# A second round for m and its transpose in the far lanes of a Newton-Schulz kernel, and side queues that skip finished entries

## The chip, the cores and the metric

The kernel runs on one core of a Trainium2 chip. The metric is the device time of one execution in microseconds; lower is better.

## The reference, cut to what matters

The input x is 32 images of 32 channels of 128 x 128. Layer 0 takes a group norm of x, then five steps of a Newton-Schulz iteration for the matrix square root of every one of the 1024 matrices A, and adds the result to x. Layer 1 takes a group norm of that, a spectral convolution on the lowest 32 modes, and adds again.

```
Y = A / norm(A);  Z = I
for _ in range(5):
    T = 0.5 * (3 I - Z @ Y);  Y = Y @ T;  Z = T @ Z
x = x + Y * sqrt(norm(A))                  # layer 0, A = group_norm(x)
F = real(fft2(group_norm(x)))              # layer 1
F = einsum over input channels of F[low modes] with weights1, weights2
x = x + real(ifft2(F, zeros elsewhere))
```

## The kernel before

The kernel doesn't run the five steps as written: `newton` (L388 to L411) computes the same kind of polynomial with two quartic stages and a last product. Its unit is a **quad**: four channels of one image, four 128 x 128 matrices side by side in a tile of 128 x 512 fp32. There are 256 quads. One product of a quad (`products`, L298) is four fp32 matrix products, which the trace shows as 8 matmul records; `transposed` (L304) shows as 4.

**One quad.** `quartic` computes v = products(mb, m) and then q = products(v, w), where w is v transposed plus r. In `newton` the first quartic gives q; then y = products(q, m); then the new m = products(q, y); then mb, the transpose of m, and r = mb + identity; then the second quartic; then two products (L298 names them m,q and y,q), the product named q,t, and the last one, y,t, which is added to xt (L410). ACT copies y, m, mb and t from PSUM (`taken`, L267). DVE makes v, q and the second t (`plus`, L273). POOL makes r (L285) and, in far lanes, w (L376).

**Two ways to transpose v.** In images 1 to 19 ("far", `is_far`) DVE transposes 32 x 32 blocks (L360), SP stores the tile to DRAM (L362), loads it in the order wanted (one load in the first quartic, L373; four in the second, L370), and POOL adds r. In the other images ("near") PE transposes v. The far way saves PE work and takes longer. 152 quads are far, 104 near.

**Rounds and lanes.** All of this is unrolled in Python, and the order of the program is the order in which it is written. `newton` is a generator; each `yield` ends a step. The main loop goes in rounds, and in each round each of seven lanes takes one step of its quad. A far quad has 20 steps, and a new one starts every `FAR` = 20/7 rounds, so that all seven lanes are in use; a near quad has 13, starts every 13/4 rounds and uses four lanes. Each engine takes its instructions in the order of the program, so that the number of rounds between a product and the product that uses it decides how much work of other quads lies between them.

**Side work.** Between the lanes' steps the loop gives one turn a round to each of several queues of generators, through `step`: `preps` (statistics of the next image, at lane 1), `specs` (spectrum of a finished image, lane 2), `posts` (`settle`, which stores a finished quad and folds it, and `forward`, the first Fourier transform, lane 3), `prods` (products with the weights) and `backs` (`inverse`, lane 0; `backs` has no turn in every fifth round for most of the time). `norms` (the normalization of the next quad) has a turn before each lane. Images are grouped in 21, 8 and 3 (`GROUPS`); the products of a group start when its last image has its spectrum, and the inverses follow. `step` runs the first generator of a queue up to its next `yield`; a generator that has nothing left to do is taken off the queue, and that uses up the turn.

**Buffers.** `four` gives out tiles by tag in turn; far quads have some more (`rooms`: first number, and what far quads have in addition).

Of the kernel before, what the change touches and what calls it, by code (L numbers as in the profile page):

```python
# [36 lines left out]
C = 32  # L37
G = 16
LANES, LESS = 7, 4
FAR, NEAR = 20 / 7, 13 / 4  # L40
GROUPS = (21, 8, 3)


# [22 lines left out]
def conv_preact_kernel(  # L66
# [74 lines left out]
    def bank():  # L141
        return ps8.tile([P, 4, P], F32, tag="ps", name="ps")
# [111 lines left out]
    def four(tag, far):  # L254
        n, more = rooms[tag]
        if far:
            turns[tag] += 1
            if turns[tag] % (n + more) >= n:
                return early.tile([P, 4, P], F32, tag=tag + "_early", name=tag, bufs=more)
        return sets.tile([P, 4, P], F32, tag=tag, name=tag, bufs=n)  # L260

    def taken(ps, tag, far, f=1.0):
        t = four(tag, far)
        if f == 1.0:
            nc.scalar.copy(t, ps)
        else:
            nc.scalar.mul(t, ps, f)  # L267
        return t

    def plus(ps, f, t, tag, far):  # L270

        s = four(tag, far)
        nc.vector.scalar_tensor_tensor(s, ps, f, t, ALU.mult, ALU.add)  # L273
        return s

    def blocks(t):


        return t.rearrange("p c x -> p (c x)").rearrange("p (a c j) -> p a c j", a=4, c=4)

    def plus_eye(mb, far):

        r = four("r", far)
        if far:
            nc.gpsimd.tensor_tensor(  # L285
                blocks(r).rearrange("p a c j -> p c a j"),
                mb.rearrange("p c (a j) -> p c a j", a=4),
                eye.rearrange("p c (a j) -> p c a j", a=4),
                ALU.add,
            )  # L290
        else:
            nc.gpsimd.tensor_tensor(r, mb, eye, ALU.add)  # L292
        return r

    def products(lhsT, rhs):
        ps = bank()
        for j in range(4):
            nc.tensor.matmul(ps[:, j, :], lhsT[:, j], rhs[:, j], start=True, stop=True)  # L298
        return ps

    def transposed(t):
        ps = bank()
        for j in range(4):
            nc.tensor.transpose(ps[:, j, :], t[:, j, :], ident)  # L304
        return ps

    def is_far(b):
        return 0 < b < FIRST
# [42 lines left out]
    def quartic(m, mb, r, far, wide):  # L351


        v = plus(products(mb, m), -1 / (QA * QR * QS), m, "v", far)
        if far:


            t = four("turn", far)
            form = "p c (b i) -> p b c i" if wide else "p c (i b) -> p b c i"
            nc.vector.transpose(blocks(t), v.rearrange(form, b=4))  # L360
            held = dram.tile([P, 512], F32, name="turn", tag="turn", bufs=8)
            kept(nc.sync.dma_start(out=held, in_=t.rearrange("p c x -> p (c x)")))  # L362
            yield
            w = four("w", far)
            wb = blocks(w).rearrange("p a c j -> p a (c j)")
            if wide:
                for b in range(4):
                    rows = slice(32 * b, 32 * b + 32)
                    src = held[:, P * b : P * b + P].rearrange("(a i) x -> i a x", a=4)
                    kept(nc.sync.dma_start(out=wb[rows], in_=src))  # L370
            else:
                src = held.rearrange("(a i) (b x) -> (i b) a x", a=4, b=4)
                kept(nc.sync.dma_start(out=wb, in_=src))  # L373
            yield
            yield
            nc.gpsimd.tensor_tensor(w, w, r, ALU.add)  # L376
            w = blocks(w).rearrange("p a c j -> p c a j")
        else:
            yield
            w = plus(transposed(v), 1.0, r, "w", far)  # L380
        yield
        q = plus(products(v, w), 1 / (16 * QS * QS), eye, "q", far)
        yield
        if far:
            yield
        return q

    def newton(g, sn, xt, m, mb, r, far):  # L388


        q = yield from quartic(m, mb, r, far, False)
        y = taken(products(q, m), "y", far, 1 / MS)
        yield
        m = taken(products(q, y), "m", far, MS)
        yield
        mb = taken(transposed(m), "mb", far, QR * QS / MS)
        r = plus_eye(mb, far)
        yield
        q = yield from quartic(m, mb, r, far, True)
        pw, py = products(q, m), products(q, y)  # L400
        w, y = taken(pw, "t", far, 1 / MS), four("y4", far)
        for j in range(4):
            c = 4 * g + j
            nc.scalar.mul(y[:, j, :], py[:, j, :], sn[:, c : c + 1])  # L404
        yield
        t = plus(products(w, q), -0.5 * EYE / 1.5, eye, "t", far)
        yield
        if far:
            yield
        nc.vector.tensor_tensor(xt, products(t, y), xt, ALU.add)  # L410
        yield  # L411
# [128 lines left out]
    def wide_products(i):  # L540
# [5 lines left out]
        def load(step):  # L546
            kk, h = divmod(step, 2)
            for l4 in range(4):
                rows = slice(32 * l4, 32 * l4 + 32)
                kept(nc.sync.dma_start(out=wts[h][rows, l4], in_=wk[kk, rows, h]))  # L550
            if not h:
                kept(nc.sync.dma_start(out=xks[kk % 2][:, 0:n, :], in_=xs[i][kk, :, 0:n, :]))
# [14 lines left out]
        for step in range(2 * KK):  # L567
            yield
            kk, h = divmod(step, 2)
            wt, xk = wts[h], xks[kk % 2]  # L570
            if not h:
                om = page(f"om{i}_{kk}")
            pm = bank()
            for t in range(4):
                for q in range(4):
                    nc.tensor.matmul(  # L576
                        pm[32 * q : 32 * q + 32, t, :],
                        xk[:, :, 8 * q + 4 * h + t],
                        wt[:, :, q, t, :],
                        start=True,  # L580
                        stop=True,
                    )
            nc.scalar.copy(
                om.rearrange("p (o l) -> p o l", l=L)[:, :, 16 * h : 16 * h + 16],
                pm.rearrange("p t (l o) -> p o (t l)", l=4),
            )
            if done and not h:
                store(*done)
            if h:
                done = kk, om  # L590
            if step + 2 < 2 * KK:
                load(step + 2)
# [208 lines left out]
    backs = []  # L801

    def step(queue):
        if queue and next(queue[0], queue) is queue:
            queue.pop(0)


# [60 lines left out]
    while todo or any(lanes) or posts or specs or prods or backs:  # L868
# [10 lines left out]
        for i in range(LANES):  # L879
            step(norms)  # L880
            far = todo and is_far(todo[0][0])
            room = lanes[i] is None and (far or LANES - lanes.count(None) < LESS)
            if todo and room and rounds >= due:
                due = max(due, rounds - 1) + (FAR if far else NEAR)
                while norms:
                    step(norms)
                b, g = todo.pop(0)
                xt = ready[0][0]
                lanes[i] = (b, g, xt, newton(g, made[b][3], *ready.pop(0), far))
                if stages:  # L890
                    stage()
            if lanes[i] is not None:
                b, g, xt, steps = lanes[i]
                if next(steps, lanes) is lanes:
                    lanes[i] = None
                    end(b, g, xt)
            if i == 1:
                step(preps)
            if i == 2 or tail:
                step(specs)  # L900
            if i == 3 or tail:
                step(posts)
            if i == 0 or tail:
                step(prods)
            if i == 0 and (rounds % 5 or len(ended) > B - 6) or tail and not (posts or specs):
                step(backs)
# [65 lines left out]
```

## Time and profile before

The median of three runs is 3214.82 us (3211.49 to 3221.01). The profiled execution has a span of 3216.0 us.

| engine | busy us | share |
|---|---|---|
| PE (matmul) | 2973.3 | 92% |
| DVE | 2365.3 | 74% |
| POOL | 2008.4 | 62% |
| ACT | 1716.3 | 53% |

A row of the page's groups gives line, engine, operation, output and inputs, shape and count, then busy us and the mean ns of one, then the engine's idle time before them and what ended most of it. A row of the waits gives the waiting engine, tile and line, what it waited for, the total in us, how many times, and the longest. In time, the profile falls into the far stage (from about 105 to 1780 us), the near stage (to about 3095 us; the products of the first group lie at 1900 to 2100 us, their inverses from 2050 to 2800), and a tail of about 120 us with the last group's products and inverses.

### The profile page before, as it was taken

Reading aid. Unit: us, or ns where it says so; the run is one execution under the profiler, and the core shown is the slowest. Engines: PE = TensorE matmul, PEld = TensorE weight load, DVE = VectorE, ACT = ScalarE, POOL = GpSimd, SP = SyncE. Lnnn points to the kernel's source line nnn. Section 1 sums busy time; section 2 is a strip of 40 time slices with the busy share of each in tenths; the row PEclk is TensorE's granted clock in tenths of the full one; section 3 lists DMA queues with packets and bytes.
Section 4 is the critical chain, followed back from the end, with each engine's and each line's share of the span. In section 5 each row is a group of like instructions: output and inputs, shape, how many; then the busy total and the mean of one; then the engine's idle time right before and its main releaser. Section 6 shows DMA issues by size and latency. Waiting matters only on the chain.

```text
span 3216.0 us, 78946 instructions
## 1 busy us (share of the span) xinstructions
PE 2973.3 (92%) x29440; PEld 2836.6 (88%) x29440; DVE 2365.3 (74%) x5672; ACT 1716.3 (53%) x4148; POOL 2008.4 (62%) x2312
## 2 busy tenths in 40 slices
PE   6999999999999999999999999999999998999954
PEld 6889899899999999999999998898889888999853
DVE  5787788778888887888788665577767776756645
ACT  3555555565556655565565555455555544546533
POOL 3566666666767666666676553466767767746642
PEclk9999999999999999999999999999999999999975
DMA  3466566666666666666666336765767676576667
GB/s 122 148 190 190 192 201 202 186 199 204 196 208 200 210 191 196 207 204 200 191 211 193 96 96 207 227 214 185 232 201 243 213 240 208 193 225 209 207 238 255
DMA packets 482317, 637.55 MB, mean 198 GB/s; under 512 B 97936, under 2 KB 263056, under 8 KB 481936
## 3 DMA queue, kind: packets, MB, share of 16 engines
q1 hardware_dynamic: 366448, 413.30, 40.3%
q10 hardware_dynamic: 113472, 211.86, 21.1%
q0 software_dynamic: 2016, 7.34, 0.6%
q8 instruction: 235, 3.85, 0.5%
q14 instruction: 146, 1.20, 0.1%
HBM read 398.75 MB, written 233.57 MB: 197 GB/s over the span
## 4 chain that ended last, share of the span: by engine, by line
PE 67%; DVE 13%; DMA 12%; ACT 3%; issue 2%; POOL 1%; SPq 1%; ACTq 0%; DVEq 0%; POOLq 0%
PE ps L298 55%; PE ps L304 6%; DMA xs<-in_xt 5%; DMA turn<-turn 2%; PE ps L764 1%; DMA w<-turn 1%; DVE a_st L193 1%; PE ps L442 1%; DVE turn L360 1%; DVE q L273 1%; DVE yt L781 1%; DVE v L273 1%; PE ps L576 1%; PE ps L742 1%; DVE xt L410 1%
## 5 line engine op out<-in xcount | busy, mean ns | idle before, releaser
L298 PE MATMUL ps<-w,v 128*128 128x128 f32 x4096 | 548.5, 278 | 26.4 <-POOL w L376 14.1
L376 POOL TENSOR_TENSOR w<-w,r 128x512 f32<-128x512 f32 x304 | 386.7, 1275 | 270.5 <-DMA w<-turn 222.0
L298 PE MATMUL ps<-y,q 128*128 128x128 f32 x4096 | 549.6, 278 | 3.9 <-ACT y L267 2.2
L423 POOL TENSOR_TENSOR fold<-xt 128x256 f32<-128x256 f32 x512 | 363.7, 731 | 279.2 <-DVE xt L410 262.5
L328 ACT ACTIVATE b<-b,a_off,a_scr 128x128 f32<-128x128 f32 x1024 | 463.9, 489 | 129.7 <-issue 54.8
L298 PEld LDWEIGHTS ps<-w,v 128*128 128x128 f32 x4096 | 500.5, 193 | 35.2 <-POOL w L376 20.1
L298 PEld LDWEIGHTS ps<-y,q 128*128 128x128 f32 x4096 | 504.7, 194 | 7.0 <-ACT y L267 3.3
L273 DVE SCALAR_TENSOR_TENSOR q<-ps,eye 128x512 f32<-128x512 f32 x512 | 347.0, 678 | 99.5 <-PE ps L298 97.9
L717 POOL TENSOR_TENSOR yt<-yt,d 128x512 f32<-128x512 f32 x236 | 297.9, 1289 | 188.0 <-ACT d L776 155.0
L193 DVE BATCH_NORM_STATS2 a_st<-xs 128x6 f32<-128x128 f32 x1024 | 231.8, 279 | 143.4 <-DMA xs<-in_xt 143.0
L335 POOL TENSOR_SCALAR x<-xt,a_nm,a_sc 128x128 f32<-128x128 f32 x720 | 317.8, 454 | 23.9 <-DVE a_n L222 20.8
L404 ACT ACTIVATE y<-ps,a_t_s 128x128 f32<-128x128 f32 x1024 | 292.1, 369 | 62.3 <-PE ps L298 61.5
L292 POOL TENSOR_TENSOR r<-b,eye 128x512 f32<-128x512 f32 x104 | 132.8, 1277 | 283.8 <-issue 224.6
L298 PE MATMUL ps<-m,q 128*128 128x128 f32 x2048 | 280.3, 280 | 27.9 <-DVE q L273 27.6
L298 PE MATMUL ps<-m,mb 128*128 128x128 f32 x2048 | 282.4, 282 | 19.6 <-ACT mb L267 19.6
L273 DVE SCALAR_TENSOR_TENSOR v<-ps,x 128x512 f32<-128x512 f32 x256 | 175.5, 686 | 165.0 <-PE ps L298 162.9
L273 DVE SCALAR_TENSOR_TENSOR v<-ps,m 128x512 f32<-128x512 f32 x256 | 174.7, 683 | 162.8 <-PE ps L298 162.1
L298 PE MATMUL ps<-y,t 128*128 128x128 f32 x2048 | 280.6, 281 | 6.6 <-DVE t L273 4.5
L298 PEld LDWEIGHTS ps<-m,q 128*128 128x128 f32 x2048 | 252.1, 194 | 35.4 <-DVE q L273 17.9
L360 DVE STREAM_TRANSPOSE turn<-v 128x512 f32<-128x512 f32 x304 | 277.9, 914 | 7.2
L298 PE MATMUL ps<-x,b 128*128 128x128 f32 x2048 | 275.6, 278 | 5.6 <-POOL x L335 5.6
L298 PEld LDWEIGHTS ps<-m,mb 128*128 128x128 f32 x2048 | 254.9, 196 | 27.7 <-ACT mb L267 25.0
(124 smaller groups left out, 5867.6 us busy)
## 6 DMA issues: line engine op xcount, KB each, us to landing
turn<-turn SPq DMA_DIRECT2D x304, 256.0 KB
b<-in_x ACTq DMA_DIRECT2D x256, 256.0 KB
xt<-in_xt ACTq DMA_DIRECT2D x256, 256.0 KB
xs<-in_xt ACTq DMA_DIRECT2D x256, 256.0 KB
mid<-xt SPq DMA_DIRECT2D x256, 256.0 KB
yt<-mid SPq DMA_DIRECT2D x128, 512.0 KB
out<-yt SPq DMA_DIRECT2D x108, 512.0 KB
w<-turn SPq DMA_DIRECT2D x152, 256.0 KB
```

Source lines behind the costliest of these rows:

```text
L193: nc.vector.bn_stats(st[:, 4 * i + c, :], tiles[i][:, c, :])
L273: nc.vector.scalar_tensor_tensor(s, ps, f, t, ALU.mult, ALU.add)
L292: nc.gpsimd.tensor_tensor(r, mb, eye, ALU.add)
L298: nc.tensor.matmul(ps[:, j, :], lhsT[:, j], rhs[:, j], start=True, stop=True)
L304: nc.tensor.transpose(ps[:, j, :], t[:, j, :], ident)
L328: nc.scalar.activation(t, x, AF.Identity, bias=offset[:, c], scale=scale[:, c])
L335: nc.gpsimd.tensor_scalar(m[:, j, :], xt[:, j, :], nm[:, c // 2 : c // 2 + 1], sc[:, c : c + 1], ALU.add, ALU.mult,)
L360: nc.vector.transpose(blocks(t), v.rearrange(form, b=4))
L376: nc.gpsimd.tensor_tensor(w, w, r, ALU.add)
L404: nc.scalar.mul(y[:, j, :], py[:, j, :], sn[:, c : c + 1])
L423: nc.gpsimd.tensor_tensor(f[:, :, 64 * half : 64 * half + 64], xt[:, :, 0:64], xt[:, :, 64:128], op)
L717: engine.tensor_tensor(yh, yh, d, op)
```

## The change

Three edits. In far quads the new m waits one round more before it is transposed, and its transpose mb waits one round more before it is used in the second quartic. A far quad then has 22 steps, so `FAR` becomes 22/7, which keeps seven lanes in use. And in `step`, when a generator turns out to be finished, the next one in the queue has the turn. The yields are meant to give ACT's copies of m and mb time before PE needs them; the loop in `step` is meant to keep side work going while a quad is spread over more rounds.

```
-FAR, NEAR = 20 / 7, 13 / 4
+FAR, NEAR = 22 / 7, 13 / 4
...
         m = taken(products(q, y), "m", far, MS)
         yield
+        if far:
+            yield
         mb = taken(transposed(m), "mb", far, QR * QS / MS)
         r = plus_eye(mb, far)
         yield
+        if far:
+            yield
         q = yield from quartic(m, mb, r, far, True)
...
     def step(queue):
-        if queue and next(queue[0], queue) is queue:
+        while queue and next(queue[0], queue) is queue:
             queue.pop(0)
```

More of the change, by code (lines that the diff above doesn't have):

```diff
@@ L39 @@
 LANES, LESS = 7, 4
-FAR, NEAR = 20 / 7, 13 / 4
+FAR, NEAR = 22 / 7, 13 / 4
 GROUPS = (21, 8, 3)
@@ L395, in newton @@
         yield
+        if far:
+            yield
         mb = taken(transposed(m), "mb", far, QR * QS / MS)
@@ L398, in newton @@
         yield
+        if far:
+            yield
         q = yield from quartic(m, mb, r, far, True)
@@ L803, in step @@
     def step(queue):
-        if queue and next(queue[0], queue) is queue:
+        while queue and next(queue[0], queue) is queue:
             queue.pop(0)
```

## The prediction

> **What bounds the kernel now.** I read the page first (slices, chain, costliest groups), then the windows view over the far stage, then the waits view for 100 to 1850 us alone, since the new yields stand under `if far`.
>
> ```profile
> PE   6999999999999999999999999999999998999954
> PEclk9999999999999999999999999999999999999975
> PE 67%; DVE 13%; DMA 12%; ACT 3%; issue 2%; POOL 1%; SPq 1%; ACTq 0%; DVEq 0%; POOLq 0%
> ...
> L376 POOL TENSOR_TENSOR w<-w,r 128x512 f32<-128x512 f32 x304 | 386.7, 1275 | 270.5 <-DMA w<-turn 222.0
> ```
>
> PE is busy nine tenths of nearly every slice and is 67% of the chain that ended last. The last line is the long wait that matters below: POOL waits for w, which travels through DRAM.
>
> ```profile
> 300.00:1700.00 1400.00, 1347.70 (x11977) 1298.89 (x11976) 1136.60 (x2738) 819.67 (x2022) 949.01 (x1043) 0.99 0.64 199
> ```
>
> Columns: busy us of PE, PEld, DVE, ACT, POOL, then clock, DMA share, GB/s. In these 1400 us PE is idle 52.3 us (3.7%). All that the change can win in the far stage is this idle time and the slow clock behind it.
>
> ```profile
> PE ps L298 <- ACT mb L267: 19.6, 21, 3.4
> PE ps L298 <- POOL w L376: 14.1, 17, 2.1
> PE ps L304 <- ACT m L267: 11.5, 8, 4.2
> PE ps L298 <- ACT t L267: 3.0, 2, 2.3
> PE ps L298 <- ACT y L267: 1.3, 3, 0.8
> ...
> POOL w L376 <- DMA w<-turn: 222.0, 125, 7.7
> ...
> SPq L373 <- DMA turn<-turn: 198.1, 104, 5.4
> SPq L370 <- DMA turn<-turn: 175.9, 105, 4.2
> ```
>
> Waits in total us, times, longest. The two waits aimed at, m before its transpose (L304) and mb before v (L298), are 31.1 us of PE's idle time; w is third, y next to nothing.
>
> ```profile
> 1003.32 1.16 PE L298 MATMUL ps<-m,mb 128*128 128x128 f32 x8 [0.75 <-ACT mb L267]
> ...
> 1005.92 0.70 DVE L360 STREAM_TRANSPOSE turn<-v 128x512 f32<-128x512 f32 x1
> ...
> 1006.65 5.22 SPq L362 DMA_DIRECT2D turn<-turn  x2
> ...
> 1012.04 1.77 SPq L370 DMA_DIRECT2D w<-turn  x4
> ...
> 1017.91 2.50 POOL L376 TENSOR_TENSOR w<-w,r 128x512 f32<-128x512 f32 x2
> ...
> 1020.69 1.06 PE L298 MATMUL ps<-w,v 128*128 128x128 f32 x8
> ```
>
> One v from its product to its use in q, from the timeline. Its product ended at 1004.4, w was ready at 1019.2: 14.8 us. The load at 1012.04 stood in SP's queue behind another lane's store (the second of the x2, issued at 1011.54).
>
> **What the Trainium skill says.** "TensorE: Matmul & The Clock Gate", Part 1, What's actually happening: after an idle window of some 3.4 us PE falls to half clock. The trace agrees on the half (0.50 from 624.7 to 631.5, behind the 4.2 us wait for m), but shorter stalls do it too (2.1 us at 287 and at 1171). Same page, Architectural detail, on queue depths: ACT, DVE and GpSimd queues are strict FIFO, so a waiting instruction holds what stands behind it; PE's matmuls in the trace are in program order too. "DMA: Bandwidth & Descriptors", Two DMAs through the same engine are not ordered: the issuing engine must wait for the first DMA's completion before a dependent one. Both SPq rows above are this wait. Its section Anatomy of one DMA gives some 2 us fixed; the shortest store-to-load distance in this trace is about 2.2 us.
>
> **The change, part by part.** The matmuls stay the same. What moves is the order of the steps, so I wrote that order out from the code. Before, it equals the order of PE's products in the timeline, so the new one can be trusted. A far lane has PE work in rounds 0 (v), 4 (q), 6 (y), 7 (m), 8 (transpose), 9 (v), 13 (q), 15 (two products), 16 (t), 18 (xt) of 20; afterwards 0, 4, 6, 7, 9, 11, 15, 17, 18, 20 of 22. Lanes start mostly three rounds apart, so rounds repeat in threes. Three rounds of the new order (#n is the lane):
>
> ```
> mT#1 y#2 v#4 | m#2 q#3 xt#5 pw#6 py#6 | v#1 t#6 q#0
> ```
>
> A product (8 records 0.111 us apart) takes 0.89 us, a transpose 0.44. "Cover" below is PE's work between the end of a product and the next product that needs it, averaged over the far quads; a quad is 10.0 us of PE work in both orders.
>
> - m to transpose: 2.5 us before, 6.5 after. mb to v: 2.6 before, 6.8 after. ACT's copy is ready 1.3 us after the product on average in both cases, 2.4 to 2.6 at the ninth tenth. Both waits vanish: -31 us. Three of the half-clock stretches (at 177, 625 and 1563 us, 6.8 us each) stand behind such waits: 3 x 6.8 / 2 = -10. Sum -41.
> - y to m: 3.1 before; after, only v#4 stands between in most cases: 0.89, 1.25 on average. y's copy is ready 0.72 us after the product at best, 1.2 on average, 2.2 at the ninth tenth. A shortfall of 0.4 us on average would be 152 quads x 0.4 = 61; if the copy always came at once, 0. The same sum taken over the waits of before comes out about a third too high or more, and ACT has little queued ahead of this copy in the new order, so I take 0.13: +20.
> - first product of pw to t: cover 3.5 before, 1.9 after, chain 1.2 on average: 0 to 15, I take +8.
> - v to q, twice a quad: still four rounds, but rounds are shorter. Cover 13.9 and 14.1 before, 11.2 and 10.9 after. v to w ready takes 11.6 us on average the first time and 12.6 the second (four loads instead of one; 8.5 at best). At this length every other w would be late: the mean slack of 3.2 and 2.3 us in the trace falls by about 2.9 and 3.3. With a spread of 1.5 us that is a shortfall of 1.5 us a quad or more, 230 us: the upper bound. Two things reduce it. Store to load takes 3.5 us on average but 2.2 at best, since a load often stands behind the store of another lane, as shown above; in the new order the two kinds of v are in different rounds and each load directly follows its own store. This takes about 1.1 us from both chains. And a stall of PE lengthens the other lanes' cover. With 10.5 and 11.5 us against 11.5 and 11.2, the late ones are about one in six and one in two, some 0.07 and 0.32 us a quad: 152 x 0.39 = 59, less the 14 of before: +45. Lower bound 0. Behind a waiting w on POOL stand the next lanes' r, x and fold; behind a waiting load on SP other stores. POOL is busy 68% and can catch up.
> - more stalls above 2 us bring more half clock, 3.4 to 6.8 us each at half price; four more or so: +8.
> - `while`: in the far stage posts needed 8 x 2 + 2 x 3 + 1 = 23 turns per batch of 22.9 rounds, and now 12 of 25.1. PE is full there, so stores that start earlier save nothing. In the near stage an inverse takes 6 turns instead of 7, so that of the seven `backs` of group 0 run denser and end some 23 rounds earlier; the same work on a full PE. At the end the last inverse of group 1 (batch 28) leaves the tail, where it lay beside the 22.7 us wait of PE for the last group's spectra. -5, between -15 and +10.
> - 22/7 against 20/7 keeps seven lanes. Buffers: m lives 10 rounds instead of 8, with 6 buffers at 3.14 rounds each (18.9); mb 2 of 9.4; y 11 of 22. None binds: 0.
>
> Sum: -41 + 20 + 8 + 45 + 8 - 5 = +35, so 3214.8 + 35 = 3250 us.
>
> **Rivals.** (a) Faster: the v chain shortens enough that w is no later than now and ACT copies y at once. For it: SP's blocked loads, as shown, and the largest two waits do go. Against it: the wide load's chain alone, without any queueing, adds up to 0.9 + 0.7 (DVE) + 2.2 + 1.4 (four issues) + 3.5 (landing) + 1.3 (POOL) = 10.0 us of the 10.9, with DVE's queueing (0.7 on average) still to come. Time: 3215 - 41 + 10 - 5 = 3180 to 3195. (b) Much slower: the chain doesn't shorten, because landing and not queueing is what takes the time (DMA share 0.64). Then each quad stalls until its cover is about the chain: some 0.8 to 1.0 us a quad above now, 3215 + 135 = 3350. For it: POOL already waits for w 125 times in 304. Against: stalls and queueing are in the measured chains. (c) It cancels: what m and mb give back, w and y take, 3215.
>
> **How the numbers follow.** The forecast's family (w and y take more than m and mb gave, 3225 to 3300) 0.48, (a) 0.25, (b) 0.14, (c) 0.13. So slower 0.62, same 0.13, faster 0.25. The range leaves out the best part of (a) and the worst of (b): 3188 to 3330.
>
> **What would show it.** In the far stage's waits: L304 <- m and L298 <- mb near 0 (right for the first step); w <- POOL above 45 us and more than 40 times; y near 20. POOL's wait for w above 222. PE's share in 300 to 1700 us not higher than 96.3%. The far stage's last w later than 1765 us by about 40. The near stage and tail within 15 us. I am wrong if PE's share there rises to 97% or more: then the chain through DRAM was queueing, and (a) holds.

## The result and the profile after

The changed kernel takes 3348.0 us in the median of four runs (3345.1 to 3357.6), the kernel before 3214.9 beside it: a ratio of 1.042 with a 95% interval of 1.039 to 1.044. It is 133 us slower, and lies above the range of 3188 to 3330.

The page of the changed kernel, its slices of PE and clock, and the two costliest groups of its list (products and the weight loads that go with them):

```profile
PE   6998998998889999889899899999999898999964
PEclk9999999999999999999999999999999999999985
...
L298 PE MATMUL ps<-w,v 128*128 128x128 f32 x4096 | 570.0, 283 | 155.4 <-POOL w L376 138.6
L298 PEld LDWEIGHTS ps<-w,v 128*128 128x128 f32 x4096 | 507.8, 195 | 183.6 <-POOL w L376 168.1
```

Before, PE's slices read 9 from the second on; now the first half has 8s in it. The idle time in front of one group of products, q = products(v, w), rose from 26.4 to 155.4 us, and 138.6 of it ended when POOL had finished w. (The lines below `newton` moved by four: L414 is the old L410, L427 the old L423.)

The windows view over the same 1400 us of the far stage, in the columns of the prediction (PE, PEld, DVE, ACT, POOL, clock, DMA share, GB/s):

```profile
300.00:1700.00 1400.00, 1260.33 (x10938) 1202.00 (x10937) 1034.53 (x2498) 751.92 (x1847) 866.58 (x955) 0.99 0.60 182
```

PE is busy 1260 us of 1400 instead of 1348, at the same clock, and issues 10938 matmuls instead of 11977: 9% less work in the same time. No engine has become busier. So no engine's own work sets the time here; something is late.

The waits of the changed kernel in the far stage (100 to 1950 us), PE, then POOL, then SP's queue:

```profile
PE ps L298 <- POOL w L376: 138.6, 123, 3.1
PE ps L298 <- ACT t L267: 11.2, 12, 2.6
PE ps L298 <- ACT y L267: 8.7, 11, 1.3
...
PE ps L304 <- ACT m L267: 0.2, 1, 0.2
...
POOL fold L427 <- DVE xt L414: 184.4, 88, 7.2
POOL w L376 <- DMA w<-turn: 180.6, 99, 7.6
POOL r L285 <- ACT mb L267: 121.3, 67, 4.8
...
SPq L373 <- DMA turn<-turn: 426.7, 151, 5.7
...
SPq L370 <- DMA turn<-turn: 293.4, 149, 4.5
```

The two waits that the yields were to remove are gone: m before its transpose fell from 11.5 to 0.2 us, mb before v from 19.6 to nothing. In their place stands w: 123 waits instead of 17. SP now waits for the store to land before practically every load (151 of 152 and 149 of 152; before 104 and 105).

Where the 127 us between the two profiled spans (3216.0 and 3343.2) lie can be read from the ends of the far quads' and the near quads' last add to xt:

| us | before | after | difference |
|---|---|---|---|
| far stage, to | 1784 | 1924 | +140 |
| near stage, length | 1309 | 1302 | -7 |
| tail, length | 122 | 117 | -5 |

The whole loss is in the far stage, and its weight loads' idle time explains most of it: 131 us before, 255 after, of which 168.1 ended with w (before 20.1). PE's own idle time in this stage rose less, from 72 to 180 us. The other 32 us of the 140 stand as PE's busy time (1612 us before, 1645 after, with the same number of products): in the changed kernel a product that starts after a wait spans 1.19 us in the mean, one that starts at once 1.08.

Following each of the 252 v of 126 far quads in the middle of the stage from the end of its product shows which part of the way is long (means in us; "DVE done" is the end of the block transpose, and q is when PE starts the product that needs w):

| | DVE done | store issued | first load | last load | POOL starts w | w ready | q | q at once after w |
|---|---|---|---|---|---|---|---|---|
| before, first v | 2.7 | 2.9 | 6.4 | 6.4 | 10.3 | 11.6 | 14.8 | 7 of 126 |
| before, second v | 2.4 | 2.6 | 6.1 | 7.6 | 11.3 | 12.6 | 14.9 | 16 |
| after, first v | 2.5 | 3.1 | 6.6 | 6.6 | 10.6 | 11.9 | 13.2 | 36 |
| after, second v | 2.1 | 2.3 | 4.9 | 6.3 | 12.0 | 13.2 | 13.6 | 87 |

The way did not get shorter as forecast. The first v's is as long as before. The second's store-to-load distance did shrink, from 3.5 to 2.7 us, but POOL starts w 5.6 us after the last load instead of 3.8. One such case, from the changed kernel's timeline:

```profile
983.89 1.37 SPq L370 DMA_DIRECT2D w<-turn  x3
...
984.61 1.27 POOL L285 TENSOR_TENSOR r<-mb,eye 128x512 f32<-128x512 f32 x1 [2.57 <-ACT mb L267]
985.83 1.28 POOL L376 TENSOR_TENSOR w<-w,r 128x512 f32<-128x512 f32 x1
987.09 0.89 POOL L335 TENSOR_SCALAR x<-xt,a_nm,a_sc 128x128 f32<-128x128 f32 x2
990.59 0.73 POOL L427 TENSOR_TENSOR fold<-xt 128x256 f32<-128x256 f32 x1 [2.61 <-DVE xt L414]
991.27 1.27 POOL L285 TENSOR_TENSOR r<-b,eye 128x512 f32<-128x512 f32 x1
992.50 0.73 POOL L427 TENSOR_TENSOR fold<-xt 128x256 f32<-128x256 f32 x1
993.18 1.29 POOL L376 TENSOR_TENSOR w<-w,r 128x512 f32<-128x512 f32 x1
...
994.52 1.16 PE L298 MATMUL ps<-w,v 128*128 128x128 f32 x8 [1.17 <-POOL w L376]
```

The last load of this w was issued at 984.8. Where POOL waits for nothing but these data, it starts 3.3 us after the last load of a first w and 4.3 us after that of a second one (means of 70 and 29 cases in this trace), so the data were there at about 989; that is an estimate. POOL began to add r at 993.2, because its queue had a fold first that waited 2.6 us for an xt, then another r and another fold. PE, which can do nothing else until then, waited.

### The profile page after: what moved, and what is told of

It is laid out like the page before. It is cut to its first block, busy times and chain, and to the rows that moved or that the text cites. A ratio compares the mean times of both kernels' runs of the same rounds, so it can differ in the third digit from the quotient of the medians.

```text
span 3343.2 us, 78733 instructions
## 1 busy us (share of the span) xinstructions
PE 3005.0 (90%) x29440; PEld 2852.4 (85%) x29440; DVE 2352.4 (70%) x5664; ACT 1714.4 (51%) x4148; POOL 2015.1 (60%) x2320
## 5 line engine op out<-in xcount | busy, mean ns | idle before, releaser
L298 PE MATMUL ps<-w,v 128*128 128x128 f32 x4096 | 570.0, 283 | 155.4 <-POOL w L376 138.6
L298 PEld LDWEIGHTS ps<-w,v 128*128 128x128 f32 x4096 | 507.8, 195 | 183.6 <-POOL w L376 168.1
L427 POOL TENSOR_TENSOR fold<-xt 128x256 f32<-128x256 f32 x512 | 365.1, 730 | 353.3 <-DVE xt L414 301.5
L267 ACT ACTIVATE mb<-ps 128x512 f32<-128x512 f32 x256 | 153.2, 598 | 599.0 <-PE ps L304 563.8
L721 POOL TENSOR_TENSOR yt<-yt,d 128x512 f32<-128x512 f32 x244 | 307.7, 1286 | 193.7 <-ACT d L780 148.0
L298 PE MATMUL ps<-q,t 128*128 128x128 f32 x2048 | 275.9, 278 | 11.3 <-ACT t L267 11.2
L298 PE MATMUL ps<-x,q 128*128 128x128 f32 x2048 | 277.6, 279 | 2.2 <-DVE q L273 2.2
```

Of the source, the lines that this page charges most:

```text
L427: nc.gpsimd.tensor_tensor(f[:, :, 64 * half : 64 * half + 64], xt[:, :, 0:64], xt[:, :, 64:128], op)
L721: engine.tensor_tensor(yh, yh, d, op)
```

## The experiments

Two theories were put against each other. **A**: a round lasts as long as the work in it; a far quad's work is spread over 22 rounds instead of 20, so that the four rounds of v's way to q hold 11 us of PE's work instead of 14, and the way through DRAM, at 12 to 13 us, no longer fits. **B and C**: the way would fit, but w is held on POOL by what stands ahead of it, folds (B) or r and the rest (C).

Each run was timed beside the kernel before, whose own median moved between 3207 and 3215 us, so that a difference of some 10 us between two rows counts only if their intervals are apart. "Wait" is PE's waiting for w in the far stage, from the one profile of each run; where the trace puts the idle time in front of q = products(v, w) down to the store, to PE, to DVE or to issue, that is taken in. "Cover" is PE's work between the product of v and its q, first and second quartic, from the order of the steps.

| run | median us | ratio to before (95%) | wait for w, us | cover, us |
|---|---|---|---|---|
| changed kernel | 3348.0 | 1.042 (1.039 to 1.044) | 139 | 11.2, 10.9 |
| e1 only the edit of step | 3227.5 | 1.005 (1.003 to 1.007) | 22 | 14.0, 14.0 |
| e2 only the yields and 22/7 | 3375.1 | 1.053 (1.049 to 1.057) | 127 | 10.9, 11.2 |
| e3 fold later | 3331.2 | 1.039 (1.035 to 1.042) | 126 | 10.9, 11.1 |
| e4 eight lanes | 3254.3 | 1.015 (1.011 to 1.019) | 73 | 14.4, 14.0 |
| e5 r later | 3408.0 | 1.059 (1.056 to 1.061) | 159 | 11.2, 10.9 |
| e6 r and fold later | 3408.8 | 1.059 (1.057 to 1.061) | 166 | 10.9, 11.1 |
| e7 eight lanes, r later | 3281.7 | 1.019 (1.016 to 1.021) | 85 | 14.4, 14.0 |
| e8 second round of m alone | 3248.6 | 1.011 (1.007 to 1.014) | 56 | 13.5, 13.2 |
| e9 second w on DVE | 3308.8 | 1.031 (1.028 to 1.034) | 65 | 11.2, 10.9 |
| e10 eight lanes, round at the load | 3148.2 | 0.981 (0.977 to 0.984) | 4 | 16.6, 16.4 |
| e11 seven lanes, round at the load | 3253.1 | 1.014 (1.010 to 1.018) | 36 | 14.0, 13.9 |
| e12 eight lanes, no second rounds | 3175.3 | 0.990 (0.987 to 0.993) | 11 | 15.7, 15.9 |
| e13 e10 without m's and mb's rounds | 3171.9 | 0.990 (0.987 to 0.993) | 4 | 17.6, 17.8 |
| e14 e10 with the old step | 3219.7 | 1.004 (1.002 to 1.005) | 0 | 16.3, 16.3 |
| e15 both w on DVE | 3307.0 | 1.033 (1.029 to 1.036) | 68 | 11.2, 10.9 |
| e16 e10 with a second round of y | 3163.0 | 0.987 (0.984 to 0.990) | 15 | 15.5, 15.8 |

**e1 and e2, each half alone.** e1 is the kernel before with

```
-        if queue and next(queue[0], queue) is queue:
+        while queue and next(queue[0], queue) is queue:
```

and e2 is the changed kernel with that line put back.

> Only the edit of step, on the kernel before. Theory A (rounds of a far quad became shorter in time, so the way of v through DRAM no longer fits): the far stage stays at 10.8 us a quad, PE waits for w about 14 us, and the near stage and the tail give what they gave in the changed kernel, some 13 us: about 3202 us. Theory B (the edit of step puts the folds close behind their xt in POOL's queue and so holds w): PE's wait for w in the far stage rises to 50 us or more and the time to 3240 or more.

> The two yields and 22/7 with the old step. Theory A: all of the loss and none of the gain at the end, about 3360 us, PE's wait for w 130 us or more. Theory B: folds come later in POOL's queue (the work of PE between xt and its fold is 8.2 us instead of 4.7), PE's wait for w falls to half, about 3290 us.

The loss comes with the yields and 22/7 (e2: 5.3%), as A has it. B expected half of the wait for w in e2, where folds come later; it stayed at 127. The edit of `step` costs 0.5% by itself (w waits 22 us instead of 14, m 18 instead of 12) and takes 27 us off together with the yields; the changed kernel's far stage ends within 4 us of e2's (1924 and 1920), and its near stage and tail are 34 us shorter.

**e3, the fold later.**

```
     def settle(b, g, st, xt):
+        if is_far(b):
+            yield
```

> The changed kernel, with settle one turn later in far quads, so that 8.6 us of PE's work lie between xt and its fold instead of 4.7. Theory A: no change, 3348 within 10 us. Theory B: POOL no longer waits for xt ahead of the second w, PE's wait for w falls from 139 us to 100 or less, and the time by 40 us or more, to 3308 or less.

17 us faster by the medians, but the intervals of the two ratios overlap; so it is a small gain at most, far from B's 40. The first w came sooner (ready after 10.7 us instead of 11.9), the second did not (13.3): POOL's folds still waited for their xt, 260 us in all, ahead of the second w.

**e4, eight lanes.** With eight lanes and 22/8 a new quad starts every 2.75 rounds, and a round holds as much work as before the change.

```
-LANES, LESS = 7, 4
-FAR, NEAR = 22 / 7, 13 / 4
+LANES, LESS = 8, 4
+FAR, NEAR = 22 / 8, 13 / 4
```

> The changed kernel with eight lanes and 22/8: the number of rounds between two quads is 2.75, as short as before the change, so the cover of v to q goes back from 11.2 and 10.9 us to 14.4 and 14.0, and that of y to m from 1.2 to 3.0, while m and mb keep their second round. Theory A: PE's wait for w falls below 40 us and the waits for m and mb stay near 0: 3190 to 3220 us. Theory B: w stays late, since folds stay close behind their xt (6.7 us of PE's work): 3260 or more.

94 of the 133 us came back. But PE still waited 73 us for w, twice A's bound, and the time is nearer to B's forecast than to A's:

```profile
PE ps L298 <- POOL w L376: 50.1, 27, 4.6
PE ps L298 <- ACT t L267: 23.4, 21, 2.3
PE ps L298 <- DMA turn<-turn: 22.5, 7, 4.1
```

Here the mean cover tells too little. With a new quad every 2.75 rounds the lanes don't lie evenly. In the trace 50 of the 252 w were ready only after PE's other work between v and q had run out, and all 50 belong to the first or the fifth quad of an image. In 33 of them that work was below 12.5 us; in the other 17 it was 12.7 to 15.3 us, and the way itself had grown to 13.8 to 16.5. So A holds for the larger part, and what makes the way longer for the rest isn't settled by this run.

**e5 to e7, r later.** POOL's r <- mb waited for ACT 121 us. These runs issue it one round later, behind the second yield; e6 adds e3's edit, e7 has eight lanes.

```
         mb = taken(transposed(m), "mb", far, QR * QS / MS)
-        r = plus_eye(mb, far)
+        if not far:
+            r = plus_eye(mb, far)
         yield
         if far:
             yield
+            r = plus_eye(mb, far)
```

> The changed kernel, with POOL's r = mb + identity issued one round later, behind the second yield. Theory A (the way of v through DRAM is longer than the shortened rounds cover): r is not on that way, no change, 3348 within 12 us. Theory C (POOL takes its work in order, and the second w is held on POOL by what stands ahead of it: r, which now waits for a transpose that PE makes late, then the first w, x, the other r and two folds): r no longer waits for ACT (121 us before), POOL runs ahead, and the time falls by 30 us or more, to 3318 or less.

> Both: r one round later and settle one turn later in far quads. Theory A: as with the fold alone, 3331 within 12 us. Theory C: the two moves add up, 3300 or less, and the distance from the last load of the second w to its start on POOL falls from 5.6 us to below 4.5.

> Eight lanes and 22/8 with r one round later. With eight lanes PE still waited 73 us for w, 23 of it directly for the store through DRAM, and POOL's r waited 0.6 us a quad for ACT. Theory A: no change from 3254. Theory C: r stops waiting, PE's wait for w falls by 20 us or more, to 3235 or less.

e5 is 60 us slower than the changed kernel, against both forecasts; e6 is no better, and e7 is 27 us slower than e4. r's own wait for ACT did shrink (from 121 to 38 us in all), but at its new place it often stands right ahead of the second w, which then begins 6.0 us after its last load instead of 5.6. This spoke against the form of C that I had and for its core: what stands between the landing of the data and w on POOL counts, and A alone, for which r plays no part, can't explain it. The half-clock time of the far stage rose too, from 38 to 113 us, which at half speed is worth about 37 us of the 60.

**e8, half a dose.** The second round for m alone, 21 steps, 21/7.

> The changed kernel with the second round for m alone: 21 steps, 21/7. Cover of v to q 13.5 and 13.2 us (before 13.9 and 14.1, changed 11.2 and 10.9), of y to m 3.0, m to transpose 5.2, mb to v 3.3. Theory A: the loss goes with the cover, so nearly all of it is gone: PE's wait for w 20 to 40 us, for m near 0, for mb about 10: 3195 to 3230. Theory C: depends on where r and the folds fall; with r still directly behind the transpose about half of the loss, 3270.

A cover of 13.2 to 13.5 us leaves a wait for w of 56 us (50.1 behind POOL, 6.3 behind the store), more than A's 40, and 1.1% of loss; the time lies between both forecasts. With seven lanes the order is that of the cover: 14 us of wait at 14 in the kernel before, 56 at 13.3, 139 at 11. Eight lanes (e4) don't fall into it.

**e9 and e15, POOL taken off the way.** The add that completes w goes to DVE, the second alone (e9) or both (e15).

```
-            nc.gpsimd.tensor_tensor(w, w, r, ALU.add)
+            (nc.vector if wide else nc.gpsimd).tensor_tensor(w, w, r, ALU.add)
```

> The changed kernel with the add that completes the second w (152 of 304) on DVE instead of POOL. Theory A (the way through DRAM itself is longer than the cover): the landing of the last load, some 10 us after the product, stays, and POOL's 1.3 us become 0.7 on a DVE that is busy 74%; w stays late in most cases: 3320 or more. Theory C (the second w is held on POOL behind folds and r for nearly 2 us after it has landed): the second w is ready 1.5 us or more earlier, PE's wait for w falls from 139 us to 70 or less, the time to 3285 or less.

> The changed kernel with both adds of w on DVE, so that nothing on POOL stands before a w. Theory A (the way through DRAM): the first w still comes too late in a third of the quads and the second in more than half, PE's wait for w 50 us or more: 3285 to 3310. Theory C (POOL's queue): PE's wait for w below 25 us, 3260 or less.

Each takes back 30 to 40 of the 133 us. The waits of e15, all far:

```profile
PE ps L298 <- DVE w L376: 33.5, 34, 1.8
...
PE ps L298 <- ACT t L267: 22.0, 21, 2.2
PE ps L298 <- PE ps L298: 17.6, 33, 0.9
PE ps L298 <- issue: 16.4, 10, 2.6
```

In front of q = products(v, w), 33.5 us ended with DVE's w and another 34 with what the trace assigns to PE or to issue, 68 together: with no POOL on the way at all, half of the 139 us remain, as A forecast. Both w of a quad are now ready 11.9 us after the product of v, so that the second, at 13.2 in the changed kernel, no longer takes longer than the first. So both theories hold a part: about half of the wait is the way through DRAM, half POOL's order. The split isn't clean, as DVE is busy 88% in e15 and other products then wait for it (t 22 us instead of 11).

**e10 to e12, a longer cover.** e10 has eight lanes and one round more between the load of w and its add in both quartics (24 steps, 24/8). e11 is that with seven lanes and 24/7. e12 is e1 with eight lanes and 20/8.

```
             yield
             yield
+            yield
             nc.gpsimd.tensor_tensor(w, w, r, ALU.add)
```

> The changed kernel with one round more between the load of w and its add in both quartics (24 steps) and eight lanes (24/8): cover of v to q 16.6 and 16.4 us, y to m 2.7, m to transpose 5.3, mb to v 6.5, t 3.1, each longer than before the change or about as long. Theory A: all waits of the far stage fall below 10 us each, the far stage ends at about 1740 and the time is 3165 to 3190. Theory C: POOL has the same work ahead of the second w; PE's wait for w stays above 40 us, 3210 or more.

> The same round at the load with seven lanes (24/7): v to q 14.0 and 13.9 us, as long as before the change; but y to m 1.8 (0.3 in a tenth of the quads), t 2.4. Theory A: PE's wait for w goes back to 20 to 40 us, that for y rises to 30: about 3235. Theory C: w waits 80 us or more, 3290.

> The kernel before with the edit of step and eight lanes, 20/8, no second rounds: v to q 15.7 and 15.9 us, m to transpose 2.9, mb to v 3.1, y to m 2.9. Theory A: PE's wait for w falls from 14 us to 5 or less, those for m and mb stay at about two thirds of 31 us: 3185 to 3205. Theory C: a wait for w of 15 us or more, no faster than 3210.

POOL is busy 7.2 to 7.3 us a quad in all of them, as in the changed kernel. With the cover back at 14 us (e11) the wait for w falls from 139 to 36; with 16.5 (e10) it is gone. e11 is the cleaner test, with as many lanes as the changed kernel and a way that is no shorter: w is ready 12.8 and 13.3 us after the product (11.9 and 13.2 in the changed kernel). So the longer cover alone takes away most of the wait. In e10 C's forecast failed as well, but that run doesn't separate the two theories, since the way got shorter there too (10.9 and 11.4 us; POOL starts the second w 3.5 us after its last load instead of 5.6). The waits of e11:

```profile
PE ps L298 <- ACT y L267: 37.3, 42, 3.1
PE ps L298 <- POOL w L377: 35.9, 30, 2.9
```

The waits and the window of e10:

```profile
PE ps L298 <- ACT y L267: 14.6, 20, 2.1
PE ps L298 <- ACT t L267: 14.1, 13, 2.5
...
PE ps L298 <- POOL w L377: 3.6, 2, 3.2
```

```profile
300.00:1700.00 1400.00, 1374.06 (x12340) 1329.64 (x12339) 1180.13 (x2827) 841.32 (x2074) 973.28 (x1071) 1.00 0.66 205
```

PE is busy 98.1% (before 96.3%), at full clock; the far stage ends at 1736 us instead of 1784. e10 beats both kernels, by 1.9% against the one before. e11 shows the price of seven lanes: the cover of y to m is 1.8 us there, and y waits 37 us. e12 shows that half of e10's gain needs no second round at all, only the eighth lane (e12 has the edit of `step` too, which alone was a loss in e1).

**e13, e14 and e16, what is in e10.** e13 leaves out the second rounds of m and mb (22/8), e14 has the old `step`, e16 adds a second round for y (25/8).

> The kernel with eight lanes and the round at the load, without the second rounds of m and mb (22 steps, 22/8): v to q 17.6 and 17.8 us, m to transpose 2.5 (0.0 in a tenth), mb to v 3.0. If those rounds gain what the profile of before promised (31 us of PE's waits and some slow clock), this is 25 to 45 us slower than the 3148 with them: 3173 to 3193, with waits for m and mb of 20 us or more together. If they gain nothing by themselves: 3148 within 8.

> Eight lanes, all the rounds, and the old step. If skipping finished entries helps by bringing side work earlier in the near stage and the tail, as e2 against the changed kernel has it: 20 to 30 us slower than 3148. If it only moves work about: 3148 within 10. If folds close behind their xt cost, as in e1: up to 15 us faster.

> Eight lanes, the round at the load, m and mb, and a second round for y (25/8): y to m 5.8 us instead of 2.7, v to q 15.5 and 15.8, t 2.6 instead of 3.1. Theory A: PE's wait for y (15 us) goes, those for t (14) and w (4) rise by some 10 together: 3148 within 10. If a cover of 15.5 us is short of the way through DRAM, w waits 30 us or more: 3170 or more.

e13 is 24 us slower than e10, but not where the yields are: its far stage ends at 1741, 5 us later, with waits of 17 us for m and mb together; its near stage is 22 us longer, and why wasn't found. So the rounds that the change adds gain some 5 us of far stage where w has room, too little to be sure of with one profile of each. e16 is 15 us slower than e10: y no longer waits, but PE waits 15 us in front of q = products(v, w), more than e10's 4. In e14 the far stage is 54 us longer than e10's:

```profile
PE ps L204 <- DVE a_qs L199: 50.3, 21, 3.6
```

This is a small product of the statistics of the next image (`prep`). With the old `step` it reaches PE before DVE has made its input, 21 times, and half-clock time rises from 10 to 61 us. `step` shifts where each turn falls among the lanes; that such shifts cost or gain 50 us was seen, which turn it was wasn't tried.

## Why the prediction was wrong

- **m and mb: right.** 31.1 us expected to vanish, 30.9 did. The 10 us for slow clock behind them did not come: half-clock time in the far stage is 41 us before and 38 after.
- **y to m: right in kind, too high.** +20 expected, 1.3 rose to 8.7. ACT's copy is ready 0.80 us after the product on average instead of 1.20, so the short cover of 0.89 mostly suffices.
- **t: right.** +8 expected, 3.0 rose to 11.2; that it was met to the microsecond is luck, as +8 was the middle of 0 to 15.
- **v to q: this step failed.** The mechanism was the right one, the term was +45 us and measured +124 on PE (14.1 to 138.6), +148 as the weight loads show it. I had worked out an upper bound of 230 and then came down to 45, because both chains were to become 1.1 us shorter. What the runs showed in its place: the first chain kept its length (11.6 to 11.9 us), the second grew (12.6 to 13.2) although its load left 0.8 us earlier relative to its store. Two sentences failed. "This takes about 1.1 us from both chains": SP's load waited for the store to land nearly every time, and for the first v the distance stayed at 3.5 us without another lane's store in the way. (The shortest distance in the trace of before is 2.0 us, not 2.2; the sum doesn't hang on it.) And "POOL is busy 68% and can catch up": POOL takes its work in order, and in the new order the pieces ahead of the second w, r and the folds, wait for PE's own later steps (121.3 and 184.4 us in the view above). e9 and e15 show that POOL's place on the way makes up about half of the wait; e11 shows that, with a way no shorter than in the changed kernel, 3 us more of cover take away most of it.
- **Clock +8: wrong, but small.** No more half clock than before.
- **`while` -5: right in the sum, by luck.** Near stage and tail are 12 us shorter together. But e2, which has the yields without the loop, needs 1453 us for them, 21 more than the kernel before; so, by one profile of each, the loop was worth 34 us there, and the yields cost 21 that the prediction did not have. That the two would interact (e1 slower, e2 slower than with it, e14) was not seen.
- **The rivals.** The time is that of rival (b), 3350, to which I gave 0.14. Its reason, that landing and not queueing takes the time, holds for the first v alone; for the second it was queueing, at a place where I hadn't looked.

## What to carry to other kernels

In a schedule of rounds, one more round for one result removes its wait, but with the same lanes it makes every other distance shorter in time. So first look for the result with the longest way and see what it has left. If it has little, add a lane (or what else is in flight) with the step. A mean of slack isn't enough for the sum (e4), and a chain through several in-order queues should not be shortened on paper because one of its links gets shorter: the next queue in line can take it all.

## What the runs showed that I had not expected

- A shorter store-to-load distance (3.5 to 2.7 us) gave nothing for the second w, since POOL started it 1.9 us later after its last load.
- Moving a piece of POOL's work by one round (e5) cost 60 us with the same instructions.
- The edit of `step` alone, which only decides in which round side work is issued, was worth +17 us (e1), -27 (changed kernel against e2) and -72 (e10 against e14).
- An eighth lane, with no other buffer, gave 1.0% together with the edit of `step` (e12; 1.5% against e1, which has that edit alone), and 6.0% on the changed kernel with the round at the load (e10: 3148 against 3348).
